# Layer 0 of a fused two-layer kernel: query loads, division steps, weight steps, group norm and a last addition moved in the queues

## The chip, the cores and the metric

The kernel runs on 1 core of one Trainium2 chip, in one launch. The metric is the device time of one execution in microseconds. Before the change the median of 3 runs is 2915.74 us (2914.01 to 2921.61).

## The reference, cut to what matters

Two layers work on x of shape (8, 384, 32, 32), that is 8 images of 384 channels and 1024 positions. The change touches only layer 0, whose core is this:

```python
tokens = gn(x).reshape(b, c, n).transpose(0, 2, 1)            # group norm, n = 1024
qkv = (tokens @ qkv_w + qkv_b).reshape(b, n, 3, 8, 48)        # 8 heads of 48
attn = einsum('bhnd,bhmd->bhnm', q * 48**-0.5, k) + relative_bias
out = einsum('bhnm,bhmd->bhnd', softmax(attn), v)
x = x + out.reshape(b, n, c) @ proj_w + proj_b
```

Layer 1 (attention with 6 heads, then a binarized feed-forward part) follows it.

## The kernel before, in words

**Tiling.** Layer 0 takes the images one after another. The heads form 4 pairs, two heads of 48 rows at partitions 0 and 64 of one tile. The fourth pair's rows lie in the spare 16-row strips of the first three, so that projections have three "blocks" of keys and three of queries. `BLOCKS0` orders them (0,keys), (0,queries), (1,keys), (1,queries), (2,keys), (2,queries). Here they are called blocks 0 to 5.

**Products in parts.** From image 1 on every product is made from operands split in a high and a low half (`h`, `l`, and `m`, `km`, `xd` for mixtures)[...]. Class `Ahead` makes the next image's blocks: for block n TensorE computes `pm` (L171, from `xd`) and then `pg` (L171, from `xh` and `xl`) in PSUM. `take(n)` is ScalarE's `t<-pm` (L677), `add` is VectorE's `t<-pg,t` (L683). `halves` is ScalarE's `h<-t` (L696), three DMAs of `h` from ScalarE's queue to the DRAM tensor `halves` (one at L701 of 512 KB, two at L703 of 64 KB), VectorE's `t<-t,h` (L697, the low half, here "the subtraction") and the same DMAs of the low half from SyncE's queue (SP). The halves of block n are made in the turn of block n + 1, before that block's `add`.

**Scores.** `Batches.run(n)` is one of 16 batches of an image (4 per pair). It issues four score tiles `s` of six products each (L920), adds the bias and takes the exponential (`e<-s,grow` on VectorE L927, `e<-e` on ScalarE L931), and weighs the values with the batch before (L893). `between` holds all that is put beside a batch: loads, and `later.step()`, twice a batch. In batch 0 it holds also `project_out` of the image before, 36 products `pp` (L997).

**Queries and keys of the next pair.** They are loaded from `halves` into SBUF by SP (L748), keys in 12 DMAs in the first batch of a pair (`at == 0`), the second half's queries in the same batch, the next pair's first queries in the third (`at == 2`). For the first pair the tiles come from SBUF: `move` fills (L719) copy strips between `h`, `l`, `m` and `km` with DMAs on SP.

**Division.** `divide(b, pair)` divides by the sums of the exponentials in steps put into the queue `later`: rows of sums to DRAM (L955), to 128 partitions (L957), the inverse with GpSimd's power (L958), to DRAM (L962), spread by `rb<-rd` (L970, two DMAs of 256 KB), GpSimd's multiplication (L974); for the fourth pair `spread_rows` moves its rows to their strips (six DMAs `oT<-oT`, L986). `project_out` reads the result.

**What sets the order.** Each engine works through its own queue in order. The order of calls and `later.after(k, work)` (after k steps) is made by hand. Which buffer of a pool a tile gets, and so what it waits for, is settled when the kernel is built: the pool `a_qk` has 9 buffers for all `h`, `l`, `t`, `xd`, `k` and `q` tiles, and PSUM has 4 tiles of two banks. Every DMA of SP and ScalarE takes one of eight completion counters in turn, over both queues together, and the built program lets a DMA wait until the one that had the same counter before it has landed.

Of the kernel before, what the change touches and what calls it, by code (L numbers as in the profile page):

```python
# [22 lines left out]
ALU = mybir.AluOpType  # L23
# [4 lines left out]
P = 128  # L28
QP = P // 2
B, C, IH, IW = 8, 384, 32, 32  # L30
N = IH * IW
# [9 lines left out]
NF0 = NP0 - 1  # L41
# [61 lines left out]
BLOCKS0 = [(0, 1), (0, 0), (1, 1), (1, 0), (2, 1), (2, 0)]  # L103
# [97 lines left out]
class _Weights:  # L201
# [15 lines left out]
    def add(self):  # L217
        for k in range(1, KC):
            self.nc.gpsimd.tensor_add(self.mean, self.w[:, 0] if k == 1 else self.mean, self.w[:, k])
# [56 lines left out]
def _layer0(tc, ins, x1, sums, shared, weights, beside):  # L276
# [4 lines left out]
    nc = tc.nc  # L281
# [4 lines left out]
    with ExitStack() as ctx:  # L286
# [14 lines left out]
        later = _Later()  # L301
# [25 lines left out]
        for g in range(P // QT):  # L327
            at = g * QN
# [550 lines left out]
        class Batches:  # L879
# [26 lines left out]

                return finish

            def run(self, n, between):

                pair, h, g = n // 4, n // 2 % 2, n % 2
                name = f"{self.b}_{pair}_{h}_{g}"
                k, q = self.halves.k[pair], self.halves.q[pair, h]
                ss, es = [], []

                def products(i):
                    ss.append(mm2(f"s{name}_{i}"))
                    for m, (a, c) in enumerate(((0, 0), (0, 1), (1, 2))):
                        for j in range(2):
                            nc.tensor.matmul(  # L920
                                ss[i][:, j], k[c][ts(j, S0), ts(BT * g + i, P)],
                                q[a][ts(j, S0)], start=(m == 0), stop=(m == 2),
                            )

                def take(i):
                    e = etile(f"e{name}_{i}")
                    nc.vector.tensor_add(  # L927
                        e.rearrange("p (j q) -> p j q", j=2), ss[i],
                        near(2 * pair, BT * g + i, h, [GW * IW, 2]),
                    )  # L930
                    nc.scalar.activation(e, e, AF.Exp)  # L931
                    es.append(e)

                for i in range(3):
                    products(i)
                take(0)
                products(3)
                for i in range(1, 4):
                    take(i)
                finish = self.weigh() if self.held else None  # L940
                self.held = pair, h, g, es
                between()
                if finish is not None:
                    finish()

        def divide(b, pair):


            o = oT[:, pair]
            sd = dram.tile([2, N], F32, tag="sd", name=f"sd{b}_{pair}")  # L950
            rd = dram.tile([2, N], F32, tag="rd", name=f"rd{b}_{pair}")
            mine = sums[:, b, pair]
            inv = kept.tile([P, 2 * N // P], F32, tag="inv", name=f"inv{b}_{pair}", bufs=2)
            for j in range(2):
                nc.sync.dma_start(sd[j : j + 1], oT[j * S0 : j * S0 + 1, pair])  # L955
            with nc.allow_non_contiguous_dma(reason="sums"):
                nc.sync.dma_start(mine, sd.rearrange("j (p c) -> (j p) c", c=2 * N // P))  # L957
                nc.gpsimd.tensor_tensor(inv, mine, over.to_broadcast([P, 2 * N // P]), ALU.pow)  # L958

            def keep_inverse():  # L960
                with nc.allow_non_contiguous_dma(reason="sums"):
                    nc.sync.dma_start(rd.rearrange("j (p c) -> (j p) c", c=2 * N // P), inv)  # L962

            later.after(2, keep_inverse)
            rb = []

            def spread():
                rb.append(kept.tile([P, N], F32, tag="rb", name=f"rb{b}_{pair}"))
                for j in range(2):
                    nc.sync.dma_start(rb[0][ts(j, S0)], rd[j].partition_broadcast(S0))  # L970
                later.after(4 if pair == NF0 and b + 1 < B else 2, multiply)

            def multiply():
                nc.gpsimd.tensor_mul(o, o, rb[0])  # L974
                if b == B - 1:
                    if pair < NF0:
                        for j in range(2):
                            nc.gpsimd.memset(oT[j * S0 : j * S0 + SP, pair], 0.0)
                elif pair == NF0:
                    later.after(2, spread_rows)  # L980

            def spread_rows():
                for c in range(NF0):
                    for j in range(2):
                        row = j * S0 + SP + c * FR
                        nc.sync.dma_start(oT[j * S0 : j * S0 + SP, c], oT[row : row + FR, pair])  # L986

            later.after(2 if pair == NF0 else 3, spread)

        pps = {}  # L990

# [85 lines left out]
        for k, at in enumerate(((17, 20, 22), (21, 25, 26), (27, 30, 31))):  # L1077
            for when, stage in zip(at, cut_weights_v(k)):
                later.after(when + 1, stage)
        xn = ahead = cuts = res = held_halves = None  # L1080
        for b in range(B):

            def beside_unit(i):
                nonlocal xn, ahead, cuts, res
                if i == (16 if b == 0 else 1) and b + 1 < B:
                    xn = load(b + 1)
                    for at, stage in zip(
                        (2, 3, 4, 6, 9, 10, 11) if b == 0 else (5, 7, 9, 13, 16, 16, 16),
                        group_norm(b + 1, xn),
                    ):  # L1090
                        later.after(at, stage)
                if i == 1 and b > 0:
                    project_out(b - 1, res, range(NF0))
                if b == B - 1:
                    for at, work in beside:
                        if at == i:
                            work()
                later.step()
                if i == (28 if b == 0 else 26) and b + 1 < B:
                    cuts = _Cut(  # L1100
                        nc, cut, BLOCKS0,
                        shared.pool.tile([P, KC * 3 * C], F32R, tag="w", name=f"wc{b}"),
                    )
                    for n in range(BB):
                        cuts.load(n)
                if b in (1, 2, 3) and i == 12:
                    t = shared.weights(f"cw{b}")
                    t = {name: t[:, ts(n, 2 * C)] for n, name in enumerate(("cl", "ch", "cd"))}
                    weights.load_part(b - 1, t["cl"])
                    for at, stage in enumerate(weights.cut(b - 1, t["cl"], t.__getitem__)):  # L1110
                        later.after(4 + at, stage)
                masks = (28, 29, 31) if b == 0 else (25, 27, 29)
                if b + 1 < B:
                    if i == masks[0]:
                        ahead = Ahead(b + 1, xn)
                    if i in masks:
                        ahead.mask(masks.index(i))

            if b == 0:
                held = []  # L1120
                for i, u in enumerate(units):
                    done = held.pop(0) if len(held) == LAG else None
                    held.append(
                        (u, scores(b, qk, u, lambda: weigh(b, *done) if done else None))
                    )
                    beside_unit(i)

                def weigh_held():
                    finish = weigh(b, *held.pop(0))
                    if finish is not None:  # L1130
                        finish()
            else:
                batches = Batches(b, ahead)
                halves = ahead
                for n in range(len(units) // 2):

                    def between(n=n):
                        pair, at = divmod(n, 4)
                        if n == 0:
                            held_halves()  # L1140
                        if at == 0:
                            if pair > 0:
                                halves.load_q(pair, 1)
                            if pair < NF0:
                                halves.load_k(pair + 1)
                        elif at == 2 and pair < NF0:
                            halves.load_q(pair + 1, 0)
                        for i in range(2 * n, 2 * n + 2):
                            beside_unit(i)

                    batches.run(n, between)

            if b + 1 == B:
                batches.weigh()()
# [36 lines left out]
            for n in range(2, len(BLOCKS0)):  # L1191
# [2 lines left out]
                add, halves = ahead.take(n)  # L1194
                if held_halves is not None:
                    held_halves()
                add()
                held_halves = halves
                if n == BB - 1:
                    cuts.load(n + BB)  # L1200
                    ahead.project_v(0)
# [1359 lines left out]
```

## Time and profile before

| What | us |
|---|---|
| the profiled execution, whole | 2915.66 |
| its span, first to last instruction | 2913.9 |
| TensorE busy | 2872.1 |
| VectorE busy | 2021.0 |
| ScalarE busy | 1553.2 |
| GpSimd busy | 496.2 |
| layer 0, from the first image's start | about 1342 |
| one image of layer 0 (images 2 to 6) | about 160 |
| mean granted TensorE clock | 0.998 |

The profiled execution lies 0.08 us under the median of the runs. The profile's first part gives busy time by engine. Its lists of waits give, for each engine and line, what ended its idle time: "PE s L920 <- DVE t L683" is TensorE standing still ahead of the scores until VectorE's addition had freed something. In the timelines a bracket behind an instruction is the idle time ahead of it, and what ended it.

### The profile page before, as it was taken

How to read it: one execution, taken by the hardware profiler on the slowest of the kernel's cores; microseconds unless marked ns; L12 is line 12 of the kernel's file. 1: busy time of each engine (PE TensorE's matmuls, PEld its weight loads, DVE VectorE, ACT ScalarE, POOL GpSimd, SP SyncE). 2: the span in 40 equal slices, each digit the busy share in tenths (PEclk: the TensorE clock that was granted, in tenths of full speed). 3: DMA queues.
4: the chain of work that ended last, by engine and by line, in shares of the span. 5: the costliest groups of instructions: out<-in, count | busy, mean ns of one | idle time of the engine just before them, and what ended most of it. 6: DMA issues, size and time to landing. Idle time of an engine off the chain costs nothing.

```text
span 2913.9 us, 43514 instructions
## 1 busy us (share of the span) xinstructions
PE 2872.1 (99%) x16850; PEld 1649.1 (57%) x16850; DVE 2021.0 (69%) x2041; ACT 1553.2 (53%) x1888; POOL 496.2 (17%) x318
## 2 busy tenths in 40 slices
PE   8999999999999999999999999999999999999999
PEld 3455464646465564654546647657647647655553
DVE  3886868687776778673756865865875875865756
ACT  2655646364554647362734655555555555564644
POOL 3120202111120202022102203202202202211020
PEclk9999999999999999999999999999999999999999
DMA  7656575665646474753301212112112112112111
GB/s 194 197 161 205 136 235 138 193 172 163 196 143 197 116 242 106 224 143 109 110 24 31 84 32 73 68 32 72 68 32 73 68 32 73 68 41 84 40 46 39
DMA packets 177751, 324.78 MB, mean 111 GB/s; under 512 B 75744, under 2 KB 94672, under 8 KB 176256
## 3 DMA queue, kind: packets, MB, share of 16 engines
q1 hardware_dynamic: 167552, 299.88, 35.6%
q10 hardware_dynamic: 9984, 22.02, 2.4%
q8 instruction: 137, 2.24, 0.3%
q14 instruction: 78, 0.64, 0.1%
HBM read 227.50 MB, written 80.65 MB: 106 GB/s over the span
## 4 chain that ended last, share of the span: by engine, by line
PE 67%; DVE 4%; DMA 3%; ACT 2%; issue 1%; SPq 0%; ACTq 0%; POOL 0%; DVEq 0%
PE s L1913 11%; PE o L1962 11%; PE o L893 8%; PE s L920 7%; PE y2p L2207 6%; PE y1p L2156 5%; PE pv L1850 4%; PE pg L171 3%; PE pp L997 3%; PE pp L2059 3%; PE pm L171 2%; PE pq L1702 2%; DVE qk L1783 1%; DMA rb<-rd 1%; PE sum L1989 1%
## 5 line engine op out<-in xcount | busy, mean ns | idle before, releaser
L931 ACT ACTIVATE e<-e 128x1024 f32<-128x1024 f32 x448 | 473.5, 1058 | 328.7 <-DVE e L927 304.4
L927 DVE TENSOR_TENSOR e<-s,grow 128x1024 f32<-128x1024 f32 x448 | 516.9, 1216 | 88.6 <-PE s L920 83.6
L1924 ACT ACTIVATE e<-s,kc 128x512 f32<-128x512 f32 x768 | 463.9, 694 | 171.8 <-PE s L1913 162.3
L1913 PE MATMUL s<-qk,qk 64*64 64x512 f32 x3072 | 419.9, 592 | 0.7 <-DVE oT L1972 0.4
L1962 PE MATMUL o<-e,v 64*64 64x512 f32 x3072 | 415.5, 590 | 0.0
L893 PE MATMUL o<-e,v 128*64 128x512 f32 x1792 | 407.7, 598 | 0.8 <-DVE e L927 0.8
L1939 DVE TENSOR_TENSOR t<-t,e 128x1024 f32<-128x1024 f32 x192 | 230.9, 1221 | 46.3 <-ACT e L1924 46.3
L1913 PEld LDWEIGHTS s<-qk,qk 64*64 64x64 f32 x3072 | 155.5, 132 | 189.3 <-issue 107.5
L920 PE MATMUL s<-q,k 64*128 64x512 f32 x2016 | 256.9, 398 | 4.3 <-DMA q<-halves 3.1
L1962 PEld LDWEIGHTS o<-e,v 64*64 64x64 f32 x3072 | 162.0, 133 | 166.7 <-issue 136.7
L893 PEld LDWEIGHTS o<-e,v 128*64 128x64 f32 x1792 | 120.3, 136 | 233.2 <-issue 216.3
L920 PEld LDWEIGHTS s<-q,k 64*128 64x128 f32 x2016 | 183.6, 184 | 110.2 <-issue 30.4
L958 POOL TENSOR_TENSOR inv<-sums,over 128x16 f32<-128x16 f32 x32 | 93.4, 2918 | 787.4 <-DMA sums<-sd 637.1
L2143 DVE TENSOR_REDUCE parts<-y 128x1 f32<-128x1024 f32 x75 | 89.7, 1217 | 103.5 <-ACT y L2140 103.1
L1936 DVE TENSOR_TENSOR t<-e,e 128x1024 f32<-128x1024 f32 x96 | 114.2, 1224 | 58.3 <-ACT e L1924 58.3
L1819 POOL TENSOR_TENSOR hc<-hc,rsqrt 128x32 f32<-128x32 f32 x24 | 138.9, 5787 | 2.0
L2059 PE MATMUL pp<-oT,L_attn_proj_wT 128*128 128x512 f32 x288 | 126.3, 595 | 2.3 <-DVE oT L2025 2.3
L1850 PE MATMUL pv<-wv,bx 128*128 128x384 f32 x384 | 128.3, 491 | 0.0
L997 PE MATMUL pp<-oT,wp 128*128 128x512 f32 x288 | 126.6, 598 | 1.3 <-issue 1.3
L1850 PEld LDWEIGHTS pv<-wv,bx 128*128 128x128 f32 x384 | 119.4, 314 | 9.8 <-ACT e L1924 4.1
L974 POOL TENSOR_TENSOR oT<-oT,rb 128x1024 f32<-128x1024 f32 x32 | 77.4, 2418 | 241.8 <-DMA rb<-rd 113.3
L2156 PE MATMUL y1p<-lun,w 128*128 128x512 f32 x360 | 113.5, 396 | 2.7 <-DVE lun L2106 2.7
(242 smaller groups left out, 4231.5 us busy)
## 6 DMA issues: line engine op xcount, KB each, us to landing
rb<-rd SPq DMA_DIRECT2D x110, 256.0 KB
wc<-cut SPq DMA_DIRECT2D x42, 576.0 KB
k<-halves SPq DMA_DIRECT2D x84, 192.0 KB
wc<-there SPq DMA_DIRECT2D x25, 576.0 KB
halves<-h ACTq DMA_DIRECT2D x28, 512.0 KB
halves<-t SPq DMA_DIRECT2D x28, 512.0 KB
xn<-in_x_dram SPq DMA_DIRECT2D x24, 512.0 KB
res<-in_x_dram SPq DMA_DIRECT2D x24, 512.0 KB
```

What stands on the lines that cost most here:

```text
L893: nc.tensor.matmul(po[ts(j, S0)], v[:, BT * g + i, 2 * pair + j, :], es[i][:, ts(j, HALF)], start=(i == 0), stop=(i == BT - 1),)
L920: nc.tensor.matmul(ss[i][:, j], k[c][ts(j, S0), ts(BT * g + i, P)], q[a][ts(j, S0)], start=(m == 0), stop=(m == 2),)
L927: nc.vector.tensor_add(e.rearrange("p (j q) -> p j q", j=2), ss[i], near(2 * pair, BT * g + i, h, [GW * IW, 2]),)
L931: nc.scalar.activation(e, e, AF.Exp)
L997: nc.tensor.matmul(pps[b, m][:, h], (wp[:, k] if k < NF0 else wl)[:, ts(m, P)], oT[:, k, ts(h, HALF)], start=(k == 0), stop=(k == (NF0 if ...
L1850: nc.tensor.matmul(pv[:, i, 0:C], xt[:, k].rearrange("c (p m) -> c m p", m=MT)[:, 2 * m2 + i], wv[:, k], start=(k == 0), stop=(k == KC - 1),)
L1913: nc.tensor.matmul(s[j][ts(c, QP), i], qk[pair, 1][rows, ts(4 * m2 + 2 * i + c, QP)], qk[pair, 0][rows, ts(h, HALF)], start=True, stop=True,)
L1924: nc.scalar.activation(e[:, ts(i, HALF)], s[j][:, i], AF.Exp, scale=kc[:, pair, j, m : m + 1])
L1939: nc.vector.tensor_add(total[j], total[j], e)
L1962: nc.tensor.matmul(po[ts(j, D1), r], v[keys, 2 * m2 + i, at : at + D1], es[j][keys, ts(i, HALF)], start=(m2 == 0 and i == 0), stop=(m2 == ...
L2059: nc.tensor.matmul(pps[m][:, h], wp[:, k, ts(m, P)], oT[:, k, ts(h, HALF)], start=(k == 0), stop=(k == NP1 - 1),)
L2156: nc.tensor.matmul(py[m][:, h], w1[:, k, ts(m, P)], un[k][i][:, ts(h, HALF)], start=(k == 0 and i == 0), stop=(k == KC - 1 and i == 1),)
```

## The change

Five things are moved; no arithmetic is added or removed.

1. The next pair's first queries are loaded in the second batch of a pair, not in the third.
2. Division: the inverse (with its load of the sums) is itself a step, one later, except for the last image, the first three pairs of image 0, and the fourth pair; the steps behind it move with it. For the fourth pair the spread `rb<-rd` comes 5 steps after the start, not 2; the multiplication 7, not 6; `spread_rows` stays at 8.
3. The last two of the four steps that cut layer 1's weights (images 1 to 3) come one batch later.
4. The three last steps of the group norm for the next image come two steps later (images 1 to 6).
5. The last block's `add` is not called in its turn, but in batch 0 of the image's scores, behind the first bias addition. Its `later.step()` goes with it.

```diff
-            def run(self, n, between):
+            def run(self, n, early, between):
...
                 take(0)
+                early()
                 products(3)
...
-                nc.sync.dma_start(mine, sd.rearrange("j (p c) -> (j p) c", c=2 * N // P))
-                nc.gpsimd.tensor_tensor(inv, mine, over.to_broadcast([P, 2 * N // P]), ALU.pow)
+            def invert():
+                with nc.allow_non_contiguous_dma(reason="sums"):
+                    nc.sync.dma_start(mine, sd.rearrange("j (p c) -> (j p) c", c=2 * N // P))
+                    nc.gpsimd.tensor_tensor(
+                        inv, mine, over.to_broadcast([P, 2 * N // P]), ALU.pow
+                    )
...
-            later.after(2, keep_inverse)
+            if b == B - 1 or b == 0 and pair < NF0:
+                invert()
+                at = (2, 2 if pair == NF0 else 3, 2, 0)
+            elif pair == NF0:
+                invert()
+                at = 2, 5, 2, 1
+            else:
+                later.after(1, invert)
+                at = 3, 4, 2, 0
+            later.after(at[0], keep_inverse)
...
-                later.after(4 if pair == NF0 and b + 1 < B else 2, multiply)
+                later.after(at[2], multiply)
...
-                    later.after(2, spread_rows)
+                    later.after(at[3], spread_rows)
...
-            later.after(2 if pair == NF0 else 3, spread)
+            later.after(at[1], spread)
...
-                        (2, 3, 4, 6, 9, 10, 11) if b == 0 else (5, 7, 9, 13, 16, 16, 16),
+                        (2, 3, 4, 6, 9, 10, 11) if b == 0 else (5, 7, 9, 13, 18, 18, 18),
...
-                    for at, stage in enumerate(weights.cut(b - 1, t["cl"], t.__getitem__)):
-                        later.after(4 + at, stage)
+                    for at, stage in zip((4, 5, 8, 9), weights.cut(b - 1, t["cl"], t.__getitem__)):
+                        later.after(at, stage)
...
-                        elif at == 2 and pair < NF0:
+                        elif at == 1 and pair < NF0:
                             halves.load_q(pair + 1, 0)
...
-                    batches.run(n, between)
+                    batches.run(n, held_add if n == 0 else lambda: None, between)
...
+                held_halves = halves
+                if n == len(BLOCKS0) - 1:
+                    held_add = add
+                    break
                 add()
-                held_halves = halves
```

## Prediction

> **What bounds the kernel now.** I read the busy times first, then TensorE's waits within layer 0, then the chain of waits at one image's end, then the granted clock behind one such end.
>
> ```profile
> PE 2872.1 (99%) x16850; PEld 1649.1 (57%) x16850; DVE 2021.0 (69%) x2041; ACT 1553.2 (53%) x1888; POOL 496.2 (17%) x318
> ```
>
> TensorE computes for 2872.1 of 2913.9 us. The change neither adds nor removes a product, so it can only win back, or add to, the 42 us in which TensorE stands still, and of those only what lies in layer 0. There the list of TensorE's waits (from 230 to 1342 us: line waiting, what it waited for, total, times, longest) gives
>
> ```profile
> PE s L920 <- DVE t L683: 7.7, 7, 2.3
> PE s L920 <- DMA q<-halves: 3.1, 5, 0.9
> PE vm L776 <- DVE v L784: 2.2, 4, 0.7
> PE pp L997 <- issue: 1.3, 6, 0.2
> PE s L920 <- DVE oT L903: 1.1, 2, 0.7
> ```
>
> Three of these rows belong to the change: the wait for the last block's addition, once at each of the seven boundaries between images; the small one ahead of `project_out` at the same place; and the wait for the next pair's queries. Together 7.7 + 1.3 + 3.1 = 12.1 us, or 0.4% of the kernel. That is the most it can win. What counts as no change is 0.3%, 8.7 us, about what the runs of this kernel can tell apart (they spread over 7.6 us).
>
> The boundary of image 4, as the chain that ended last in its window (start, length, what):
>
> ```profile
> 715.94 1.04 ACT h L696
> ...
> 717.98 3.25 DMA halves<-h
> ...
> 721.30 1.06 ACT h L696
> 722.35 0.02 issue
> 722.38 1.23 DVE t L697
> 723.60 1.15 DVE t L683
> 724.75 0.04 issue
> 724.79 0.96 PE s L920 x6
> 725.75 0.22 issue
> 725.97 1.10 PE pp L997 x2
> ```
>
> To be seen: the addition itself (1.15) is only the chain's tail. It stands behind the subtraction, which needs block 4's high half (721.30), and that waited for the landing of the DMAs of block 3's high half (715.94), which had its buffer's turn. The fourth score tile began at 724.79, where the third had ended near 724.0.
>
> **The change part by part.** The waits of each instruction I take from the two built programs, their lengths from this trace.
>
> *Queries sooner.* Before, the eight issues (3.67 us of SP's time from 323.01 in image 1) stand behind `rd<-inv`, which waits for GpSimd's power until 322.63. After, they stand right behind the rows of sums (near 314.9), some 8 us sooner, while the waits were at most 0.9. The ninth buffer of the pool is free for them, so no new wait for a buffer. I take −3.1 us, all of the row. Worst case: they land no sooner, 0.
>
> *Division's steps apart.* POOL's own order is unchanged. The inverse comes a step later, the spread comes with it, and the only reader is `project_out` of a later batch, apart from the fourth pair. There `rb<-rd` goes from ahead of three groups of fills on SP to behind the queries' halves, so SP no longer stands from 693.4 to 695.77 waiting for `rd`. The multiplication moves one step and `spread_rows` none. TensorE waits for neither row now; cover is a whole batch (some 10 us, a 16th of an image's 160). I take 0. It costs only if `oT` comes too late for `pp`, which is counted below.
>
> *Weights' steps and group norm.* Two VectorE steps (0.94 and 0.56 us) go from the tenth batch to the eleventh, both ahead of `oT` L903 whose two waits (1.1 us) come from the larger steps that stay. VectorE idles 1.02 us just there, so 0; at worst 3 images x 0.56 = 1.7. Group norm's three steps on GpSimd (1.2 to 1.5 us each) come 6.5 us later, and are read first by the masks' steps, seven steps on: 0.
>
> *The last block's addition later.* By itself this only changes the order of two VectorE instructions, e0 (1.2 us) and the addition (1.15). The fourth score tile gets its PSUM from e0 rather than from the addition, and `pp` from the addition rather than from e0. Both stand behind the subtraction, as before, so by itself nothing goes away: whichever is first, the fourth tile waits for one and `pp` for both. The row "s <- DVE t L683" will become "s <- DVE e L927" with the same length, not vanish.
>
> What does change is what it drags along, seen in the built programs at all seven boundaries:
>
> (a) The order of the requests moves the pool's buffers by one: block 3's high half gets the buffer of an `xd`, and so waits for block 5's second product `pm<-xd`, and not for DMAs that landed long ago. The six `pm` begin at 717.53 and take 1.40 us, and ScalarE's `take` sees the last at 719.13, 0.20 behind its end; the second is then seen at 717.53 + 2 x 0.23 + 0.20, about 718.20. Block 3's high half begins at 718.20 instead of 715.94: +2.26 us. All that hangs on it moves: its DMAs are issued at 719.27 and not at 717.01.
>
> (b) The completion counters shift: the last fill on SP (`l<-h`), which the first score tile's fourth product needs, now waits for the landing of block 3's large DMA. A lone DMA of this size lands in 2.73 us (block 5's, issued 731.32, released 734.05), so 719.27 + 2.73 = 722.00; the fill itself I put at some 2 us (8 KB of sums landed in 1.83, 64 KB in at most 2.39): about 724.0. The fourth product would be due at 722.28: TensorE waits near 1.7 us there, before the first tile is done.
>
> (c) `spread_rows`' six DMAs on SP wait for counters of block 3's and block 4's high halves; the last of them now also ends up behind block 4's large DMA, and is needed by the third pair of products of `pp` (1.74 us behind its start).
>
> The sum at the fourth score tile, two paths. Path A, the chain above with the later start: 718.20 + 1.04 = 719.24; its DMAs land about 3.3 us later (3.25 for the row above, 3.3 with the issues) 722.57; block 4's high half 1.06, 723.65; subtraction 1.23 with its hand-over, 724.79; e0 1.2, then the tile at 726.06, or 8.53 us behind the start of block 5's products. Path B, the late fourth product: first tile ends near 724.55, later tiles 0.7 to 0.8 each: they are done by the time of A, so the two do not add; A decides. The seven images' offsets now are 8.10, 7.52, 7.59, 7.26, 8.95, 7.45 and 7.35, mean 7.75. So +0.78 each, +5.5 us in all. I do not add the whole 2.26, because five of the seven have the landing of block 3's DMAs take longer than a lone one (from the end of one high half to the start of the next: 5.16, 4.57, 4.64, 4.32, 5.99, 4.49, 4.39, against 3.3): the other DMAs of that moment (block 2's) will be through when it starts later. With the same contention as now it would be +2.26 each, +15.8; with none and an earlier e0, near 0. For (c) I take 0.2 x 7 = +1.4 (0 to 0.6 each).
>
> Sum: 2915.66 − 3.1 + 5.5 + 1.4 = 2919.5 us; the profiled execution stands 0.08 under the median, so nothing is added.
>
> *A rule against a row.* In image 5 the wait is the longest, and the slices around it show the granted clock (ninth number of a line, behind the five engines):
>
> ```profile
> 884.00:887.00 3.00, 0.81 (x8) 0.34 (x4) 2.29 (x3) 0.68 (x1) 0.00 (x0) 1.00 0.58 194
> 887.00:890.50 3.50, 3.38 (x9) 1.60 (x10) 3.50 (x5) 2.12 (x3) 0.00 (x0) 0.53 0.60 197
> 890.50:894.00 3.50, 3.50 (x9) 1.59 (x8) 1.44 (x2) 3.04 (x3) 0.00 (x0) 0.98 0.62 218
> ```
>
> TensorE stood 2.31 us before 887.12, and for the 3.5 us that followed it had 0.53 of its clock, which cost some 1.27 us beside the wait (`pp` took 16.64 in place of 15.69, the tile before it 1.50 in place of 1.18). The Trainium skill, "TensorE: Matmul & The Clock Gate", section "Part 1: The HAM clock gate (the "warmup" mystery)", has the clock drop only after a whole idle window of about 3.4 us. By the rule gaps of 1.7 us cost only themselves. By the row a gap of 2.31 was enough; one of 1.46 (image 1) left the clock at 1.00. If the new gaps count like image 5's, 7 x 1.27 = 8.9 us, less the 1.27 already there: +7.6. I take 0, since 1.7 is nearer to 1.46 than to 2.31, but (b)'s gap and the fourth tile's lie close together and may add up in one window, so the other end stays in the range.
>
> **The rivals.**
> *The clock drops at the boundaries* (slower): the gaps of (b) and of the fourth tile together pass the point between 1.46 and 2.31 us at all seven boundaries: 2919.5 + 7.6 = 2927. For: image 5. Against: six of seven gaps now leave the clock at one.
> *The landing takes as long as now* (slower by more than 0.3%, the point being +12 us at the seven ends together): block 3's DMAs, though issued 2.26 us later, meet the fills and `spread_rows`, and each boundary loses all of it: 2915.7 − 3.1 + 15.8 + 2.5 = 2931. For: the 5.16 and 5.99 of images 1 and 5. Against: the lone landing.
> *The change does nothing*: the late high half is covered because the landing is shorter by what it starts later, and the queries gain little: 2914.5 (2915.7 less a part of 3.1).
> *The wait at the boundary goes* (faster): if the addition was what held the tile, 2915.7 − 7.7 − 1.3 − 3.1 = 2903.6. Against it: subtraction and landing stand ahead of e0 just as of the addition.
>
> **How the numbers follow.** Likeliest, 2919.5 with its own range of 2914 to 2924: 0.48. Clock: 0.22. Full landing: 0.12. Nothing: 0.12. Faster: 0.06. Slower by over 0.3% (above 2924.5) are the clock, the landing: 0.34. Faster (under 2907): 0.06. The rest, 0.60, is the same. The range 2913 to 2930 leaves out the fast case, and about half of the full landing.
>
> **What would show it.** In the changed profile: "s L920 <- DMA q<-halves" gone; "s L920 <- DVE t L683" replaced by "s L920 <- DVE e L927" and by a wait for `l<-h`, each seven times, together above 12 us; ScalarE's `h` L696 waiting for TensorE's `pm` L171; `pp` waiting for `oT` (c). Slices behind the boundaries at a clock near 0.5 would show the first rival. I am wrong if the sum of TensorE's waits for scores falls: then the high half's wait was not on the path.

## The result, and the profile after

The changed kernel takes 2916.51 us (median of 12 runs, 2912.11 to 2921.21) where the kernel before, run beside it, takes 2916.89 (12 runs, 2912.0 to 2921.61): ratio 1.0001, 95% interval 0.9993 to 1.001, or between 2 us faster and 3 us slower. The forecast was 2919.5 (2913 to 2930), most likely "the same". The profiled execution took 2915.22 us, with a span of 2913.4.

The busy times after:

```profile
PE 2872.4 (99%) x16850; PEld 1648.2 (57%) x16850; DVE 2010.5 (69%) x2041; ACT 1554.4 (53%) x1888; POOL 492.7 (17%) x318
```

TensorE's hardly moved. VectorE's fell by 10.5 us though it runs the same 2041 instructions; the prediction had no reason for that. TensorE's waits in layer 0 after (230 to 1342 us, columns as before: total, times, longest):

```profile
PE s L920 <- DMA l<-h: 10.3, 6, 1.8
PE s L920 <- DMA oT<-oT: 1.7, 1, 1.7
PE o L893 <- DVE e L927: 1.2, 5, 0.3
PE vg L776 <- DVE t L683: 0.9, 2, 0.5
PE pp L1011 <- issue: 0.8, 4, 0.2
PE s L920 <- DVE oT L903: 0.2, 1, 0.2
```

The waits for queries (3.1 us) are gone, as forecast. So are those for `v` (2.2 in this window, 3.0 with one ahead of it), which was not. The 7.7 us for the addition were replaced by 12.0 us at the same seven places (the first two rows; the second is image 4's, put down to `oT` for want of a nearer event). These are the fill's 1.7 us each that the prediction gave. At image 4's end:

```profile
712.16 1.56 PE L171 MATMUL pm<-xd,wc 128*128 128x512 f32 x6
712.83 1.05 ACT L696 CAST h<-t 128x1024 fp32r<-128x1024 f32 x1 [2.15 <-PE pm L171]
...
713.91 0.34 ACTq L701 DMA_DIRECT2D halves<-h  x1
...
716.60 0.51 SPq L719 DMA_DIRECT2D l<-h  x1
...
718.93 0.49 PE L920 MATMUL s<-h,l 64*128 64x512 f32 x1 [1.75 <-DMA oT<-oT]
```

Block 3's high half waits for `pm` and begins 0.67 us behind the first of its products (forecast 0.67). Its large DMA, issued at 713.91, lands 2.7 us later, and only then SP lets the last fill go (716.60). The first score tile's fourth product stands 1.75 us for it. In the seven images the gap is 1.70, 1.71, 1.74, 1.75, 1.68, 1.75 and 1.68 us.

What came behind that gap was not in the predicted sum. The granted clock (ninth number) at image 4, then at image 3, where the gap was as long:

```profile
716.00:719.00 3.00, 1.25 (x8) 0.45 (x6) 0.85 (x2) 1.80 (x2) 0.00 (x0) 1.00 0.49 93
719.00:721.00 2.00, 2.00 (x12) 1.63 (x14) 1.95 (x3) 0.05 (x1) 0.00 (x0) 0.65 0.94 301
721.00:723.00 2.00, 2.00 (x11) 1.35 (x9) 2.00 (x2) 1.01 (x1) 0.00 (x0) 0.50 0.51 146
723.00:725.00 2.00, 2.00 (x7) 0.87 (x5) 2.00 (x3) 1.71 (x2) 0.00 (x0) 1.00 0.74 238
```

```profile
557.00:559.00 2.00, 1.76 (x15) 1.43 (x15) 1.98 (x2) 0.00 (x0) 0.00 (x0) 1.00 0.79 248
559.00:561.00 2.00, 1.78 (x11) 0.81 (x9) 2.00 (x3) 1.06 (x1) 0.00 (x0) 1.00 0.53 187
```

The ends of images 2, 4 and 6 had half the clock for some 3.4 us; those of images 1, 3, 5 and 7 kept all of it. From the first of block 5's products to `project_out` it took 9.94, 11.03, 9.99, 11.07, 9.93, 10.64 and 9.93 us (before: 9.28, 8.69, 8.77, 8.44, 10.45, 8.62 and 8.53): 72.5 against 62.8, so +9.7 us.

**Theory A**: two things in the change matter. It brings the queries in time (−3.1). And its division edit moves the fourth pair's spread, which loses at the seven ends (a buffer, a completion counter, at times the clock) and gains back waits for `v`. The last block's addition does next to nothing. **Theory B**: the loss comes from that addition, as the prediction's text had it. **Rival C**: the waits for `v` went for another reason than a changed place of GpSimd's multiplication.

### The profile page after: what moved, and what is told of

The parts are those of the page before. It is cut to its first block, busy times and chain, and to the rows that moved or that the text cites. A ratio compares the mean times of both kernels' runs of the same rounds, so it can differ in the third digit from the quotient of the medians.

```text
span 2913.4 us, 43519 instructions
## 1 busy us (share of the span) xinstructions
PE 2872.4 (99%) x16850; PEld 1648.2 (57%) x16850; DVE 2010.5 (69%) x2041; ACT 1554.4 (53%) x1888; POOL 492.7 (17%) x318
## 4 chain that ended last, share of the span: by engine, by line
PE 86%; DMA 4%; DVE 4%; ACT 2%; issue 1%; SPq 1%; ACTq 0%; POOL 0%; DVEq 0%
PE o L893 14%; PE s L1930 11%; PE o L1979 11%; PE s L920 11%; PE y2p L2224 6%; PE pg L171 6%; PE y1p L2173 5%; PE pv L1867 4%; PE pm L171 3%; PE pp L2076 3%; PE pp L1011 3%; PE vg L776 2%; PE pq L1719 2%; PE s L824 1%; PE o L855 1%
## 5 line engine op out<-in xcount | busy, mean ns | idle before, releaser
L927 DVE TENSOR_TENSOR e<-s,grow 128x1024 f32<-128x1024 f32 x448 | 517.4, 1215 | 86.6 <-PE s L920 79.8
L920 PE MATMUL s<-q,k 64*128 64x512 f32 x2016 | 254.0, 397 | 0.3 <-DVE oT L903 0.2
L961 POOL TENSOR_TENSOR inv<-sums,over 128x16 f32<-128x16 f32 x32 | 93.2, 2913 | 728.5 <-DMA sums<-sd 562.6
```

What stands on the lines that cost most here:

```text
L920: nc.tensor.matmul(ss[i][:, j], k[c][ts(j, S0), ts(BT * g + i, P)], q[a][ts(j, S0)], start=(m == 0), stop=(m == 2),)
L927: nc.vector.tensor_add(e.rearrange("p (j q) -> p j q", j=2), ss[i], near(2 * pair, BT * g + i, h, [GW * IW, 2]),)
```

## The experiments

The kernel before, run beside each group, took 2912.2, 2911.8 and 2911.3 us; ratios are to that.

| run | what | ratio (95% interval) |
|---|---|---|
| sp2 | changed, the fourth pair's spread early again | 0.9995 (0.9987 to 1.0003) |
| no5 | changed, without the addition's edit | 1.0012 (1.0005 to 1.0018) |
| only1 | before + queries sooner | 0.9988 (0.9981 to 0.9994) |
| only2 | before + division | 1.0011 (1.0004 to 1.0017) |
| only34 | before + weights' steps and group norm | 1.0012 (1.0006 to 1.0018) |
| only5 | before + addition later | 0.9996 (0.9988 to 1.0004) |
| onlymul | before + fourth pair's multiplication later | 1.0002 (0.9991 to 1.0013) |
| nomul4 | before, fourth pair's multiplication left out | one run, 2910.55 us |
| late4 | sp2, block 4's halves later instead of the addition | 0.9985 (0.9973 to 0.9996) |
| l5 | late4, spread late as in the change | 1.003 (1.0018 to 1.0042) |
| l5x | l5, x loaded two steps later | 1.0128 (1.0109 to 1.0147) |
| l2y | late4, x and its statistics two steps later | 0.9942 (0.9929 to 0.9954) |

The four parts alone give −1.2, +1.1, +1.2 and −0.4 thousandths, together +0.7 (2 us), where the whole has 0.1 (−0.7 to 1.0). But the waits for queries go in only1 and in only2 as well (their lists are below), so this gain of some 1.1 thousandths is in the sum twice. Counted once, the parts make about +1.8, above the interval of the whole, though each part has some ±0.7 of its own. That the parts add up is so not shown; the +1.2 of only34 is the one without an explanation.

**Whose is the loss at the ends: the spread's or the addition's?** First the spread alone was set back.

```diff
-                at = 2, 5, 2, 1
+                at = 2, 2, 5, 1
```

> The changed kernel with one line of the division set back: the fourth pair's spread of the inverse comes 2 steps after the start again, as before the change, and its multiplication 5 steps behind that, so that the multiplication and spread_rows stay where the change put them. Theory A (the loss at the images' ends comes from the spread's place: two DMAs fewer ahead of the fills shift completion counters and one buffer): the seven waits for l<-h (1.7 us each) go, the row of waits for VectorE ahead of the fourth score tile comes back at 7 to 8 us, the waits for q and for v stay away; 4 to 7 us faster than the changed kernel, 2909 to 2913. Theory B (the loss comes from the last block's addition behind the first bias addition): the waits for l<-h stay at about 12 us, 2916 to 2917.

Next the addition alone, put into the kernel before:

```diff
-                add()
+                if n == len(BLOCKS0) - 1:
+                    held_add = add
+                    break
+                add()
```

> The kernel before with the fifth edit alone: the last block's addition behind the first bias addition. Theory A: no wait for l<-h; the 7.7 us ahead of the fourth score tile stay and only change their name from t L683 to e L927; time within 1 us of before, 2916 to 2918. Theory B: waits for l<-h of 1.7 us at the seven ends, half clock behind some, 4 to 10 us slower than before, 2921 to 2927.

The waits of these two, sp2 first:

```profile
PE s L920 <- DVE e L927: 9.0, 7, 2.4
PE vm L776 <- DVE v L784: 2.5, 3, 1.2
PE pp L1011 <- issue: 1.1, 5, 0.2
```

```profile
PE s L920 <- DVE e L927: 8.3, 7, 2.1
PE vm L776 <- DVE v L784: 2.0, 3, 0.9
PE pp L998 <- issue: 1.5, 7, 0.2
PE s L920 <- DMA q<-halves: 1.5, 2, 0.9
```

In both the row for `l<-h` is absent, and the wait ahead of the fourth tile is back at 8 to 9 us under its new name. Theory B falls. In sp2 the waits for `v` came back with the early spread, against what theory A expected, and the time is 0.9995: some 2 us under the changed kernel's ratio, where 4 to 7 were expected. The same two questions from the other side, the changed kernel without the addition's edit (the last diff reversed), and the division's edit alone in the kernel before:

> The changed kernel with the fifth edit alone undone: the last block's addition in its turn. Theory A (the spread's place makes the waits for l<-h, the addition's place makes next to nothing): seven waits for l<-h of about 1.7 us, no waits for v, none for q, time within 1.5 us of the changed kernel. Theory B (the addition's place makes them): the waits for l<-h go, 7 to 8 us of waits for t L683 come back.

> The kernel before with the second edit alone: the division's steps. Theory A (all of the loss and of the gain in the rows for l<-h and v is here): seven waits for l<-h of 1.7 us (12 us) in place of 7 to 9 us for t L683, half clock behind some three of them, no wait for v, 35 subtractions of 1.21 to 1.23 us; waits for q fewer or gone, since the inverse now stands behind them or apart; 2 to 6 us slower than before. Rival (loss needs another edit with it): no waits for l<-h.

The waits of no5, then of only2:

```profile
PE s L920 <- DMA l<-h: 12.1, 7, 1.8
PE s L920 <- DVE oT L903: 3.2, 3, 1.9
```

```profile
PE s L920 <- DMA l<-h: 10.2, 6, 1.7
PE s L920 <- DMA oT<-oT: 1.8, 1, 1.8
```

Both have the gaps of the changed kernel, 12 us in all, and only2 neither waits for `v` nor for `q`. That settles the place. The built programs of the changed kernel, no5 and only2 make block 3's high half wait for `pm` and the last fill for block 3's large DMA; those of before, sp2 and only5 make neither wait. The traces agree: in the first three the high half begins 0.66 to 0.67 us behind the first `pm` at all seven ends, and the fill is issued as that DMA lands; in the others both come before the first `pm`. Without the addition's edit the time was not within 1.5 us of the changed kernel's ratio, but 1.0012; the two intervals overlap. The profile of no5 has half clock behind four ends instead of three, but over all executions the two kernels have the same recorded clock (mean 0.9974 for both), so that is chance of the one execution. Its 3.2 us of waits for `oT` are of the right size; no run separates them from chance.

**Why did the waits for v go?** The multiplication's step alone:

```diff
-                later.after(4 if pair == NF0 and b + 1 < B else 2, multiply)
+                later.after(5 if pair == NF0 and b + 1 < B else 2, multiply)
...
-                    later.after(2, spread_rows)
+                    later.after(1 if b + 1 < B else 2, spread_rows)
```

> The kernel before with one part of the division alone: the fourth pair's multiplication on GpSimd one step later (spread_rows where it was). Theory A (the waits for v went because this multiplication no longer runs beside block 2's subtraction): that subtraction takes 1.23 us and not 2.65 in all seven images, VectorE's busy time falls by 7 x 1.4 = 10 us, the five waits for v (3.0 us) go, all else stays; 2 to 4 us faster, 2913 to 2915. Rival C (the waits for v went since block 3's high half starts later, or through other moved steps): subtraction at 2.65, waits for v stay at 3 us, time as before.

Nothing changed (1.0002; waits for `v` 2.8 us in the window and 0.8 ahead of it). GpSimd has nothing between, and in both traces its wait ahead of the multiplication in image 4 ends with the landing of `rb` (7.60 us before, 8.51 in onlymul): one step more or less in the order of calls moved nothing. What was expected of theory A fell here, not the collision itself. So the multiplication was taken out in images 0 to 6 (the fourth pair's rows stay undivided there):

```diff
-                nc.gpsimd.tensor_mul(o, o, rb[0])
+                if pair < NF0 or b == B - 1:
+                    nc.gpsimd.tensor_mul(o, o, rb[0])
```

> The kernel before without GpSimd's multiplication of the fourth pair in images 0 to 6 (that pair's rows stay undivided there), all else as it was. The run of that multiplication one step later left it beside block 2's subtraction, which took up to 3.3 us there too, so its step is not what sets its time: it starts when the spread rows land. Theory A (the subtraction is slowed because GpSimd's multiplication runs beside it, and the waits for v follow): all 35 subtractions in 1.21 to 1.23 us, VectorE busy 2010 to 2011 us, no wait for v (0 to 0.5 us), time 2 to 4 us under before. Rival (the subtraction is slowed by the DMAs that move halves at that time): subtractions of 2.6 to 3.4 us stay, waits for v of 2 to 3 us stay.

The subtraction's 35 instances (ns, min/median/max) in the kernels before, after, onlymul and nomul4:

```profile
L697 DVE TENSOR_TENSOR t<-t,h x35: 1215/1226/3432, 205.6 to 1215.0; 128x1024 f32<-128x1024 f32 x35
```

```profile
L697 DVE TENSOR_TENSOR t<-t,h x35: 1212/1225/1226, 204.9 to 1213.1; 128x1024 f32<-128x1024 f32 x35
```

```profile
L697 DVE TENSOR_TENSOR t<-t,h x35: 1214/1226/3367, 203.3 to 1213.5; 128x1024 f32<-128x1024 f32 x35
```

```profile
L697 DVE TENSOR_TENSOR t<-t,h x35: 1212/1224/1227, 205.4 to 1210.3; 128x1024 f32<-128x1024 f32 x35
```

Without the multiplication no subtraction is slow and no wait for `v` is left; with it at the old landing, up to 3.4 us. Rival (DMAs slow it) falls, since the DMAs stayed. In the kernel before one sees the two lie over each other, in image 4:

```profile
700.65 2.39 POOL L974 TENSOR_TENSOR oT<-oT,rb 128x1024 f32<-128x1024 f32 x1 [7.60 <-DMA rb<-rd]
701.48 2.65 DVE L697 TENSOR_TENSOR t<-t,h 128x1024 f32<-128x1024 f32 x1
...
705.87 0.76 PE L776 MATMUL vm<-wx,xd 128*128 128x384 f32 x3 [0.43 <-DVE v L784]
```

The subtraction ends 1.1 us behind the multiplication's end, about the 1.23 that it takes alone, as if it had stood until then. The Trainium skill, "SBUF — State Buffer", section "🔬 SBUF: two separate sides", says this: a VectorE instruction with two SBUF inputs and a GpSimd instruction that reads SBUF take a shared pair of ports in turn, each for its whole length. The case agrees, and also in the reverse: in the changed kernel the multiplication (708.02 to 710.42) lies beside the addition `t<-pg,t`, which reads one input from PSUM, and that took 1.22 us as always.

**The other parts alone.**

```diff
-                        elif at == 2 and pair < NF0:
+                        elif at == 1 and pair < NF0:
```

> The kernel before with the first edit alone: the next pair's first queries a batch sooner. Theory A (the parts add up): no wait for q (3.1 us before), the waits at the images' ends (7 to 9 us) and for v (2 to 4 us) unchanged; 3 us faster, 0.999. Rival (the eight DMAs now sit where the second half's queries or x land, and another wait takes the place): waits of 2 to 3 us for q or k elsewhere, time as before.

0.9988 is −3.5 us (−5.5 to −1.7). Its waits:

```profile
PE s L920 <- DVE t L683: 8.6, 7, 2.6
PE pp L997 <- issue: 1.5, 7, 0.2
PE vm L776 <- DVE v L784: 0.7, 2, 0.4
```

The queries' row is gone and no other took its place. The third and fourth edits alone:

```diff
-                        (2, 3, 4, 6, 9, 10, 11) if b == 0 else (5, 7, 9, 13, 16, 16, 16),
+                        (2, 3, 4, 6, 9, 10, 11) if b == 0 else (5, 7, 9, 13, 18, 18, 18),
...
-                    for at, stage in enumerate(weights.cut(b - 1, t["cl"], t.__getitem__)):
-                        later.after(4 + at, stage)
+                    for at, stage in zip((4, 5, 8, 9), weights.cut(b - 1, t["cl"], t.__getitem__)):
+                        later.after(at, stage)
```

> The kernel before with the third and fourth edits alone: the two weights' steps a batch later, the group norm's three last steps two steps later. Theory A: nothing beyond VectorE's oT waits of about 1 us going to 0.2; waits at the images' ends, for q and for v as before; within 1 us of before. Rival (weights' steps collide elsewhere): a wait of 1 us or more for oT or e in three images, slower by 1 to 3 us.

The 1.1 us of waits for `oT` went, as expected, but the time is 1.0012, +3.5 us (1.7 to 5.2). Theory A did not expect that; the rival gave 1 to 3 us, but with a wait of 1 us or more in three images. Its profiled execution (2915.13 us) shows no new wait of that size: seven waits for the addition of 8.3 us, 3.4 for `v`, 2.5 for the queries (2.3 of it under "issue"). The recorded clock explains part at most: its 22 executions have a mean of 0.9981, the 59 of the kernel before beside it 0.9986, which is worth some 1.3 us (an estimate, the difference times 2914). Where the rest is stays open.

**What the addition's edit could have done.** Block 4's subtraction holds the fourth tile, not the addition. In sp2's kernel the addition was put back, and block 4's halves were called behind the first bias addition:

```diff
+                if n == len(BLOCKS0) - 1:
+                    held_add, held_halves = held_halves, halves
+                    add()
+                    break
                 if held_halves is not None:
                     held_halves()
                 held_halves = halves
-                if n == len(BLOCKS0) - 1:
-                    held_add = add
-                    break
                 add()
```

> The kernel of the first run here, with the fifth edit replaced: the last block's addition in its turn again, and instead block 4's halves (high half, subtraction, DMAs) called behind the first bias addition. Theory A (the fourth score tile is held by block 4's subtraction, which waits for a landing, and not by the addition): the waits ahead of the fourth score tile and of project_out at the seven ends go, some 8 to 9 us less than the first run, 2901 to 2904. Rival (something else of the same length is late there, such as the rows of oT or a PSUM tile that ScalarE frees): waits of 5 us or more at the seven ends under another name, within 3 us of the first run.

From the first tile to `project_out` all seven ends take 2.96 us (before 4.15 to 6.15), and both rows of the ends are gone. But the time is only 4.4 us under the kernel before and 0.8 under sp2, where 8 to 9 under sp2 were expected:

```profile
PE s L920 <- DMA q<-halves: 7.1, 6, 2.1
PE vm L776 <- DVE v L784: 2.8, 4, 1.1
PE s L920 <- DVE oT L903: 1.9, 2, 1.4
```

The gain came back as a wait for the second pair's first queries. Two tries followed, first with the late spread, so that the multiplication would not meet the subtraction (`at = 2, 5, 2, 1` again), and with that x later:

> The run with block 4's halves behind the first bias addition, but with the fourth pair's spread 5 steps after the start, as in the changed kernel. Its built order has no wait for a landing ahead of the last fill, since block 4's DMAs now come behind it. Theory A (a late spread keeps GpSimd's multiplication away from the subtraction): no waits at the images' ends, as in that run, subtractions all 1.21 to 1.23 us, waits for v under 0.5 us in place of 2.8, first queries of the second pair still late (5 to 8 us in all, since SP brings them behind the low halves); 2 to 4 us under that run. Rival (block 3's high half, here 2.3 us later, delays SP further): the waits for queries grow by 5 us or more, slower than that run.

```diff
-                if i == (16 if b == 0 else 1) and b + 1 < B:
+                if i == (16 if b == 0 else 3) and b + 1 < B:
...
-                        (2, 3, 4, 6, 9, 10, 11) if b == 0 else (5, 7, 9, 13, 18, 18, 18),
+                        (2, 3, 4, 6, 9, 10, 11) if b == 0 else (3, 5, 7, 11, 16, 16, 16),
```

> The kernel of the run before this, with the next image's x loaded two steps later on SP, so behind the second pair's first queries and not ahead of them (the group norm's steps stay at their times). Theory A (the gain at the images' ends comes back as waits for queries because SP brings x first): waits for q from some 7 us down to 0 to 3, 3 to 6 us faster than the run before, 8 to 12 under the kernel before. Rival (the queries' source, block 3's and 4's halves, is late, not SP's order): waits for q stay at 5 to 8 us.

In l5 the waits for `v` went, but those for `q` rose to 8.5, for VectorE's `oT` to 6.0, and `pp` waited 3.1 us for `oT<-oT`: 1.003. The rival had the sign, but gave 5 us more of waits for `q`, and they grew by 1.4. In l5x the waits for `q` did go, but VectorE stood for x:

```profile
DVE gst L514 <- DMA xn<-in_x_dram: 51.4, 6, 9.1
```

and the accumulation of the heads, behind the statistics in its queue, made TensorE wait 44.5 us. Theory A was right about SP's order and wrong about its price. So in late4's kernel x was loaded two steps later again, and the first four steps of the group norm moved with it (the last three stay where they were):

```diff
-                if i == (16 if b == 0 else 1) and b + 1 < B:
+                if i == (16 if b == 0 else 3) and b + 1 < B:
...
-                        (2, 3, 4, 6, 9, 10, 11) if b == 0 else (5, 7, 9, 13, 18, 18, 18),
+                        (2, 3, 4, 6, 9, 10, 11) if b == 0 else (5, 7, 9, 13, 16, 16, 16),
```

> The version with block 4's halves behind the first bias addition (and the spread 2 steps after the start), with the next image's x loaded two steps later on SP, behind the second pair's first queries, and the group norm's first four steps two later with it (in the run where they stayed, VectorE stood at the batch statistics until x had landed, and its accumulation of the heads behind them: 44.5 us). Theory A: waits for q from 7.1 us to 0 to 3, no long wait for VectorE's oT, no wait at the images' ends; 2903 to 2906 where the kernel before takes 2912, some 4 us under that version. Rival (the queries' source is late and not SP's order): q waits stay at 5 to 8 us, same time as that version.

All that is left of TensorE's waits from 230 to 1342 us:

```profile
PE vm L776 <- DVE v L784: 2.6, 5, 0.9
PE o L893 <- DVE e L927: 1.0, 4, 0.3
PE pq L1720 <- ACT tra L1692: 0.7, 1, 0.7
PE vg L776 <- DVE t L683: 0.3, 1, 0.3
```

2893.55 us (5 runs), ratio 0.9942 (0.9929 to 0.9954): 17 us under the kernel before, which is faster than both kernels, and more than the 6 to 9 expected. No stretch of layer 0 has a lowered clock in its trace; the mean clock of its 5 executions is 0.9994, that of the kernel before beside it 0.9986, so some 2.4 of the 17 us are clock (an estimate, as above).

## Why the prediction was right, and where it was not

*The range and the sign.* The measured time lies in the range, 3 us under the forecast, and "the same" was the likeliest case. But two large errors stood against each other, so that the number came so near is in part luck.

*Queries, −3.1.* Right: gone, and alone −3.5. What was not seen is that the division's edit takes the same row away by itself (only2), so the change has this gain once, from either edit.

*"Division's steps apart … I take 0."* This step failed, twice. The two consequences (a) and (b), the buffer and the counter, were read correctly from the built program and their sizes were right (0.67 us into the products; a gap near 1.7), but the prediction put them under the last block's addition. They belong to the division: only2 has them, only5 has not, and setting back the fourth pair's spread takes them away (sp2). And the edit has a gain that was missed: `rb` lands later, GpSimd's multiplication leaves block 2's subtraction, VectorE does 10 us less and TensorE's 3.0 us of waits for `v` go. The row was in the trace of before: one instruction with a median of 1.226 us and a maximum of 3.432.

*The addition "by itself only renames".* Right: only5, 8.3 us under `e L927`, 0.9996.

*Weights and group norm, 0.* Not right in time (+3.5 alone), and not explained.

*Path A, +0.78 each, +5.5 in all.* The mechanism was right and the size too small: +9.7 up to `project_out`. At full clock `project_out` began 9.93 to 9.99 us behind the first product, about 0.25 above the forecast offset with the tile's own 1.18. Of this 0.1 is a slip in the sum (723.65 + 1.23 is 724.88, not 724.79), and the rest a longer landing: in image 1 block 3's high half ended at 227.56 and block 4's began at 231.06, 3.5 us and not 3.3. (Before, all seven of these times were above 3.3, not five.) Nor did A decide alone: in image 1 the subtraction ended at 233.36 and the first tile, held up by the fill, at 233.30, so the wait for `e L927` that was forecast beside the fill's does not show as a row of its own.

*(c), `pp` waiting for `oT`, +1.4.* No row for it, and at six of the seven ends no sign of it; in image 5 `project_out` took 16.07 us in place of 15.69, at full clock, so some 0.4 at most.

*The clock, 0.* The step failed in three of the seven ends of the profile. There `project_out` began 0.7 to 1.1 us later than at full clock; with what it lost itself (16.16 in place of 15.69 in image 6), each cost some 1.1. Over all executions the changed kernel's mean clock is 0.9974, that of the kernel before 0.9982 to 0.9986 in the three groups of the experiments: worth 2.3 to 3.4 us (an estimate, the difference times 2914), so the first rival, at 0.22 and 7.6 us, came true in part. That 1.7 is nearer to 1.46 than to 2.31 was no argument: the last section shows that it was not the length that decided. The price of 1.27 was a little low, since 16.64 runs from start to start and 15.69 to the last end; measured alike it is 16.71 against 15.69, 1.34 in all.

*The sum.* In the two profiles −3.1 (q), −3.0 (v), −0.9 (`oT`) and −0.1 (`project_out` itself, all seven images) stand against +9.7: +2.6, where the changed kernel reached layer 1 at 1344.18 and not 1345.77 us, so −1.6. Two things fill most of the difference. The products of `s<-q,k` are busy 2.9 us less (254.0, before 256.9), beside the listed waits. And image 0, where TensorE waits for `e` near 156 us in all kernels, gave 0.7: the kernel before had half clock behind that wait (1.7 us), the changed kernel had not, but came there 1.0 us later. That is chance and no merit of the change. About 1 us is not attributed.

## What to carry to other kernels

A reordering's consequences belong to the edit that moves instructions in a shared resource (pool, completion counter, port), which need not be the edit that is named for the place: build each part alone and look which one has the new wait. Of each instruction that a step moves, look at what runs beside it on GpSimd and VectorE: a maximum far above the median in the row of an operation is worth a look; here it was a collision. The wait at the boundary went when the last thing in its chain that depends on a landing was moved (late4), and the time followed only when what this pushed back in SP's queue was moved too (l2y).

## What the hardware showed that was not expected

Half clock follows a short gap or not by where the gap falls. In the changed kernel the three stretches at 0.5 in layer 0 last 3.41 us each and begin at 395.32, 719.59 and 1043.86 us, so 324.27 us apart, which is 95 times their own length. The five of no5 also lie whole multiples of it apart (70, 26, 95 and 95). So the trace can be cut into periods of 3.41 us. These are the periods around image 4's gap (717.19 to 718.93), then around image 3's (555.50 to 557.24):

```profile
716.18:719.59 3.41, 1.67 (x11) 0.87 (x11) 1.26 (x2) 1.62 (x2) 0.00 (x0) 1.00 0.47 90
719.59:723.00 3.41, 3.41 (x19) 2.48 (x15) 3.36 (x4) 1.06 (x1) 0.00 (x0) 0.50 0.70 238
```

```profile
552.34:555.75 3.41, 3.16 (x14) 1.99 (x12) 2.25 (x2) 1.18 (x2) 0.00 (x0) 1.00 0.57 192
555.75:559.16 3.41, 1.92 (x15) 1.43 (x15) 2.37 (x3) 0.98 (x1) 0.00 (x0) 1.00 0.73 196
559.16:562.57 3.41, 3.19 (x12) 1.54 (x12) 3.41 (x5) 2.10 (x2) 0.00 (x0) 1.00 0.56 151
```

Image 4's gap lies within one period, in which TensorE is then busy for 1.67 of 3.41 us, and the next period has half the clock. Image 3's, as long, lies over the border of two, and neither is followed by it. Of the 21 gaps of 1.67 to 1.77 us at the ends in the changed kernel, no5 and only2, 11 lie within one period, and ten of them are followed by half clock (not image 4's of no5); of the ten over a border none is. The prediction's two points fit: the 2.31 us of image 5 lay within one period, the 1.46 of image 1 over a border, and so did a gap of 2.10 in only5 that was not followed either. It is the place in the period that decides here, and an idle time of half a period was enough; the rule weighed in the prediction (a whole idle window of about 3.4 us) asks for too much.

One such stretch costs at most half its length, 1.7 us: from the gap near 156 us in image 0 to the first products for image 1 the kernel before took 36.61 us with it, the changed kernel 34.91 without. At the changed kernel's ends, where TensorE waits for other things too, it cost some 1.1.
